# A fused attention and expert kernel: three loads moved to another queue, and smaller shares for background work

## The chip, the core and the metric

The kernel runs on one core of a Trainium2 chip. The core has five engines, each with its own queue of instructions that it works off in order: TensorE (PE in the profile; PEld is its loading of weights), VectorE (DVE), ScalarE (ACT), GpSimd (POOL) and SyncE (SP), which here only issues DMAs. Engines wait for each other and for DMAs through semaphores. The metric is the device time of one execution in microseconds (us), lower is better.

## The reference

Eight sequences of 1024 tokens with 256 features go through a block of causal attention with 16 heads of 16 features, and then through a layer of eight experts, of which each token takes two. Cut to what is computed:

```python
def attn(x, Wq, Wk, Wv, Wo):
    q, k, v = (heads(x @ W.T) for W in (Wq, Wk, Wv))     # 16 heads of 16
    score = where(causal, q @ k.T / sqrt(16), -inf)
    return merge(softmax(score) @ v) @ Wo.T

def ffn(h, router_w, router_b, gate_up, gate_up_b, down, down_b):
    scores = softmax(h @ router_w.T + router_b)          # 8 experts
    topk_w, topk_idx = top_k(scores, 2)
    gate, up = split(h @ gate_up[e] + gate_up_b[e])      # 256 -> 2 x 512
    act = (clip(up, -7, 7) + 1) * min(gate, 7) * sigmoid(1.702 * min(gate, 7))
    y_e = act @ down[e] + down_b[e]                      # 512 -> 256
    return sum over the two chosen experts of topk_w * y_e

x = x + layernorm(attn(layernorm(x)))
x = x + layernorm(ffn(layernorm(x)))
```

All is in float32.

## The kernel before

**Stages.** First comes `begin` (L452): it loads the first sequence (512 KB twice) and W_q, W_k by SP, W_v, W_o by ScalarE's queue (L460), normalises, transposes and projects the first sequence for the first heads, and lets `spread` (L612) copy the heads' 16 rows each into 32-row slots of `qP` and `kP` by small DMAs on SP, four for q and four for k for each half of the sequence. Then the attention runs in 32 units (8 sequences times 4 groups of 4 heads), and then 71 tiles of 256 slots, each of one expert.

**Attention.** A unit passes through two phases. In the first (`maxima_tiles`, PSUM tile `sa`) PE computes scores and VectorE reduces them to row maxima; tokens' maxima go back into a spare row of `qP` (`rows`, L652: `nm`, a transpose `nmps`, a copy `nmT` on ScalarE, four small DMAs on SP). In the second (`values_tiles`, `sb`), PE computes the scores once more, transposed, with the maximum taken off by that spare row, ScalarE exponentiates them (`pT`), GpSimd masks the edges, and PE multiplies with the values (`av`). The first phase of unit u runs beside the second of unit u-1, in 9 steps of 2 pairs of heads. So unit 0 has only the first phase. Two PSUM buffers hold the `sa` of two pairs; a step's kind is EDGE (two masked reductions with the causal mask), TWO (one reduction of a short row of blocks, and a copy of the edge blocks) or WHOLE (one reduction of 1024 columns a partition).

**Background.** All other work (normalising the next sequence, projections `pjq`, `pjk`, values `vps`, the output projection `finish`, and the way of finished tokens to the experts, `route`) is written as generators that yield pieces with costs for the four engines. `pump` gives each engine a credit (`earn`) and emits pieces while no credit they need is below zero (`affordable`). The call for unit 0 is in L1225: it grants 1.2 us of PE per pair. All engines but GpSimd keep the order that the source puts out. `finish_by` at the start of unit 1 emits what is left of the first values and projections; `finish_all` (in the loop over tiles, at tile 10) emits all that is left.

**Where the moved loads stand.** `others` (L523) is such a generator; its first part runs as soon as it is started, after `begin`. There SP issues the router's weight `rwr`, the experts' first biases `gubr`, and four copies of the router's bias `rbias`, then a fill of an empty row block and, later, the bias table. Next it emits `weights` for v and o, then the transposes `rps` (of `rwr`) and `gubps` (of `gubr`) on PE, each with a copy on VectorE.

**Routing.** `route` normalises the tokens (`xn`), transposes them (`x2ps`), multiplies with the router (`lpsT`), transposes back (`lps`), ranks the experts on VectorE, counts with two matmuls (`cps`), and scatters the tokens by 8 indirect DMAs on GpSimd into one region of DRAM per expert. After the last of the 16 token blocks `fill_tails` writes eight fills on SP and `table` computes which tile belongs to which expert (matmuls `segps`, `firstps`, `tabps`). A first table, made when four blocks are still missing, serves tiles 0 to 11 (`EARLY = 12`), so these start before the last blocks are routed; the last two blocks' `finish` and `route` run between the pieces of tiles 0 to 9.

**A tile.** `load_tile` (two tiles ahead) loads rows, weights and biases by SP. `turned` transposes the rows (`xtps`), and each of four quarters does four matmuls into `gu`, `gate` and `up` on VectorE, `sig` on ScalarE, a product on GpSimd, and `act` on VectorE, one quarter late. `lower_half` multiplies with the second weight (`dn`, after the second and the third quarter of the next tile), adds the bias (`ys`) and scatters the result by two indirect DMAs on GpSimd. `pump` is called twice in each quarter (L1310, L1321) and once after it (L1472). At the end `both` gathers, weights, normalises and stores.

Of the kernel before, what the change touches and what calls it, by code (L numbers as in the profile page):

```python
# [11 lines left out]
F32 = mybir.dt.float32  # L12
# [5 lines left out]
P = 128  # L18
# [40 lines left out]
def attn_moe_kernel(  # L59
# [15 lines left out]
    nc = tc.nc  # L75
    B, S, D = x.shape
# [10 lines left out]
    E = router_w.shape[0]  # L87
    FF = down.shape[1]
    FT = FF // P
    TB = 512  # L90
    NT = B * S // TB
    NTB = TB // P
# [44 lines left out]
        out=lower, in_=lower, compare_op=ALU.is_gt, fill=0.0,  # L137
# [270 lines left out]
    with ExitStack() as attn:  # L408
# [43 lines left out]
        def begin():  # L452

            wr = {}
            for name, w, queue, tag in (
                ("q", wq, nc.sync, "avs"), ("k", wk, nc.sync, "avs"),
                ("v", wv, nc.scalar, "aT"), ("o", wo, nc.scalar, "aT"),
            ):
                wr[name] = ap2.tile([P, KT, D], F32, tag=tag, name=f"wr_{name}")
                queue.dma_start(out=wr[name], in_=w.rearrange("(t p) i -> p t i", p=P))  # L460
            xt = xs[0]
            xnTs[0] = ap0.tile([P, KT, S], F32, tag="xnT", name="xnT_0")
            steps = [ln_steps(xt[:, ts(t, NTB), :], NTB) for t in range(NC)]

            def all_of(gen):
                while True:
                    try:
                        next(gen)
                    except StopIteration as end:
                        return end.value  # L470

            def apply(t, mv, rstd):
                shift = small.tile([P, NTB], F32, tag="shift", name="shift")
                nc.vector.scalar_tensor_tensor(
                    shift, mv[:, :, 0:1].rearrange("p n c -> p (n c)"), -1.0, rstd,
                    ALU.mult, ALU.mult,
                )
                xn = ap3.tile([P, NTB, D], F32, tag="xn", name=f"xn_0_{t}")
                for n in range(NTB):
                    of = xt[:, t * NTB + n, :]  # L480

                    if n % 2 and t == 0:
                        ln_apply(xn[:, n, :], of, mv, rstd, n)
                    else:
                        nc.scalar.activation(
                            xn[:, n, :], of, AF.Identity,
                            bias=shift[:, n : n + 1], scale=rstd[:, n : n + 1],
                        )
                return xn

            for name in ("q", "k"):
                uns[0, 0, name] = ap0.tile(
                    [P, S], F32, tag=f"un{name}0", name=f"un{name}_0_0"
                )
            fill(0)
            got = all_of(steps[0])
            for kt in range(KT):
                weights("q", wr["q"], kt)
            for _ in range(NTB // 2):
                next(steps[1])  # L500
            xn = apply(0, *got)
            got = all_of(steps[1])
            for kt in range(KT):
                weights("k", wr["k"], kt)
            for kt in range(KT):
                turn_x(0, 0, xn, kt)
            xn = apply(1, *got)
            for t in range(NC):
                if t:
                    for kt in range(KT):  # L510
                        turn_x(0, t, xn, kt)
                for name in ("q", "k"):
                    project_chunk(0, 0, name, t)
                spread(0, ts(t, QC))
            for mx in mxs:
                in_order(nc.gpsimd.memset(mx, NEG))
            for vp in vps:
                in_order(nc.gpsimd.memset(vp, 1.0))
            for i in range(1, NU):
                fill(i)  # L520
            return wr

        def others(wr):  # L523

            rwr = ap2.tile([E, D], F32, tag="xT", name="rwr")
            nc.sync.dma_start(out=rwr, in_=router_w)
            gubr = ap2.tile([E * 2 * FT, P], F32, tag="xT", name="gubr")
            nc.sync.dma_start(out=gubr, in_=gate_up_b.rearrange("e (c p) -> (e c) p", p=P))
            for n in range(NTB):
                nc.sync.dma_start(out=rbias[:, n, :], in_=router_b.partition_broadcast(P))  # L530

            nc.sync.dma_start(
                out=xs_dram[ds(E * R, TS), :].rearrange("(n p) d -> p n d", p=P), in_=zeros
            )
            for name in ("v", "o"):
                for kt in range(KT):
                    yield piece(pe=0.3, act=0.45)
                    weights(name, wr[name], kt)
            yield piece(pe=0.3, dve=0.2)
            ps = ps_b.tile([P, KT, E], F32, tag="b", name="rps")  # L540
            for kt in range(KT):
                nc.tensor.transpose(ps[:, kt, :], rwr[:, ts(kt, P)], ident[:E, :E])
            nc.vector.tensor_copy(rw32[:, :, :E], ps)
            yield piece(pe=0.2, dve=0.4)
            ps = ps_b.tile([P, E * 2 * FT], F32, tag="b", name="gubps")
            nc.tensor.transpose(ps, gubr, ident[: E * 2 * FT, : E * 2 * FT])
            bias = ap2.tile([P, E, 2 * FT], F32, tag="lgT", name="bias")
            nc.vector.tensor_copy(bias, ps.rearrange("p (e c) -> p e c", e=E))

            nc.vector.tensor_scalar(bias[:, :, FT:], bias[:, :, FT:], 1.0, None, ALU.add)  # L550
            nc.sync.dma_start(
                out=bias_dram[:, :, : 2 * FT].rearrange("e p c -> p e c"), in_=bias
            )
            for e in range(E):
                nc.sync.dma_start(
                    out=bias_dram[e, :, 2 * FT :], in_=down_b[e].partition_broadcast(P)
                )
# [577 lines left out]
        with tc.manual_schedule(  # L1135
# [11 lines left out]
            for u in range(B * NG + 1):  # L1147
# [12 lines left out]
                for k in range(K):  # L1160
# [15 lines left out]
                    for pair in range(2):  # L1176
# [45 lines left out]
                        if first and second:  # L1222
                            pump(most=0.0 if whole and not pair else 1.0)
                        elif first:
                            pump(1.2, 1.2, 0.8, 1.0)  # L1225
                        else:
                            pump(1.2, 2.0, 0.8, 1.4)
                second = values_tiles(u) if first else None
# [69 lines left out]
    def quarter(i, f, xT, wg, bs, act):  # L1298

        ps = ps_gu.tile([P, 2, TS], F32, tag="gu", name=f"gu_{i}_{f}")  # L1300
        for half in range(2):
            for kt in range(KT):
                nc.tensor.matmul(  # L1303
                    ps[:, half, :],
                    lhsT=wg[:, kt, ds(half * FF + f * P, P)],
                    rhs=xT[:, kt, :],
                    start=(kt == 0), stop=(kt == KT - 1),
                )
            if half == 0 and i + AHEAD < EARLY:
                pump(0.6, 0.5, 0.8, 0.6)  # L1310
        gt = m3.tile([P, TS], F32, tag="gate", name=f"gate_{i}_{f}")
        nc.vector.tensor_scalar(gt, ps[:, 0, :], bs[:, f : f + 1], LIMIT, ALU.add, ALU.min)  # L1312
        sg = m3.tile([P, TS], F32, tag="sig", name=f"sig_{i}_{f}")
        nc.scalar.activation(sg, gt, AF.Sigmoid, scale=ALPHA)  # L1314
        up = m3.tile([P, TS], F32, tag="up", name=f"up_{i}_{f}")
        nc.vector.tensor_scalar(  # L1316
            up, ps[:, 1, :], bs[:, FT + f : FT + f + 1], LIMIT + 1.0, ALU.add, ALU.min
        )
        in_order(nc.gpsimd.tensor_tensor(sg, sg, gt, ALU.mult))  # L1319
        if i + AHEAD < EARLY:  # L1320
            pump(0.6, 0.5, 0.8, 0.6)  # L1321

        def product():
            nc.vector.scalar_tensor_tensor(  # L1324
                act[:, f, :], up, 1.0 - LIMIT, sg, ALU.max, ALU.mult
            )

        return product
# [100 lines left out]
    with tc.manual_schedule(engines={engines.PE, engines.DVE, engines.Activation}):  # L1429
# [18 lines left out]
        for i in range(NTILES):  # L1448
# [7 lines left out]
            for f in range(FT):  # L1456
                now_left = quarter(i, f, xT, wg, bs, act)
                if left:
                    left()
                left = now_left  # L1460
                for _ in range(2 if f == FT - 1 and i % 2 else 1):
                    an_end(i)
                if f == 1 and behind:
                    next(behind)
                if f == 2:
                    if i + 1 < NTILES:
                        xTs[i + 1] = turned(i + 1, loads[i + 1][0])
                    if behind:
                        next(behind)
                        next(behind)  # L1470
                if i + AHEAD < EARLY:
                    pump(1.2, 1.0, 1.5, 1.2)  # L1472
            while ready < NT and i >= tiles_for(ready):
                waiting.append(ready)
                ready += 1
# [49 lines left out]
```

## Time and profile before

| | us |
|---|---|
| median of 3 runs | 2242.74 (2240.94 to 2247.95) |
| the profiled execution's own time | 2242.13 |
| its span in the trace | 2240.4 |
| PE busy | 2172.7 (97%) |
| VectorE busy | 1646.1 (73%) |
| ScalarE busy | 1090.1 (49%) |
| GpSimd busy | 1065.0 (48%) |

The span runs from the first to the last instruction. The profile divides it into 40 slices of 56.0 us; unit 0's first `sa` starts at 22.70 us, tile 0's `xtps` at 1413.60 us. A steady tile takes 10.80 us from one `xtps` to the next.

How to read it: a line of the timeline has the start in us, the time in us, engine, source line, operation, result and operands, shapes and count, and in brackets how long the engine had been idle before it and what released it. A line of the windows has the busy time of each engine in a stretch, the granted clock of PE as a share of full speed, and what the DMA engines did. A name like `SPq` means that SP's queue issues a DMA. float32 matmuls run as two passes, so a written matmul counts twice in the trace.

### The profile page before, as it was taken

Reading aid. Unit: us, or ns where it says so; the run is one execution under the profiler, and the core shown is the slowest. Engines: PE = TensorE matmul, PEld = TensorE weight load, DVE = VectorE, ACT = ScalarE, POOL = GpSimd, SP = SyncE. Lnnn points to the kernel's source line nnn. Section 1 sums busy time; section 2 is a strip of 40 time slices with the busy share of each in tenths; the row PEclk is TensorE's granted clock in tenths of the full one; section 3 lists DMA queues with packets and bytes.
Section 4 is the critical chain, followed back from the end, with each engine's and each line's share of the span. In section 5 each row is a group of like instructions: output and inputs, shape, how many; then the busy total and the mean of one; then the engine's idle time right before and its main releaser. Section 6 shows DMA issues by size and latency. Waiting matters only on the chain.

```text
span 2240.4 us, 45184 instructions
## 1 busy us (share of the span) xinstructions
PE 2172.7 (97%) x16801; PEld 1356.0 (61%) x16801; DVE 1646.1 (73%) x3770; ACT 1090.1 (49%) x2179; POOL 1065.0 (48%) x1229
## 2 busy tenths in 40 slices
PE   7999999999999999999999999989999999999995
PEld 4444544544445445445445444678888888888884
DVE  3766777867777877877776787676658888887775
ACT  3566665666666666666666666422112322332222
POOL 3321553573473473472482463464445444454543
PEclk8899999999999999999999999999999999999998
DMA  3101102102111111111111111575567878877773
GB/s 82 38 4 40 22 20 59 40 21 53 37 29 38 51 30 34 51 35 26 51 42 21 47 51 40 205 230 207 201 219 264 274 252 272 275 243 274 242 245 121
DMA packets 141363, 251.17 MB, mean 112 GB/s; under 512 B 17664, under 2 KB 103576, under 8 KB 139224
## 3 DMA queue, kind: packets, MB, share of 16 engines
q1 hardware_dynamic: 127640, 212.22, 30.5%
q0 software_dynamic: 12960, 35.54, 4.2%
q8 instruction: 133, 2.18, 0.4%
q14 instruction: 86, 0.70, 0.1%
q10 hardware_dynamic: 544, 0.52, 0.1%
HBM read 175.74 MB, written 55.76 MB: 103 GB/s over the span
## 4 chain that ended last, share of the span: by engine, by line
PE 83%; DVE 8%; POOL 4%; issue 2%; ACT 1%; DMA 1%; SPq 1%; ACTq 0%; DVEq 0%; POOLq 0%
PE sa L689 20%; PE gu L1303 18%; PE av L821 12%; PE dn L1334 9%; PE sb L784 7%; PE vps L582 3%; PE yps L882 3%; PE pjk L596 3%; PE pjq L596 2%; PE avt L852 1%; PE xtps L1283 1%; DVE acc L1386 1%; POOL pT L801 1%; DVE gate L1312 1%; PE aps L872 1%
## 5 line engine op out<-in xcount | busy, mean ns | idle before, releaser
L792 ACT ACTIVATE pT<-sb 128x512 f32<-128x512 f32 x1152 | 625.0, 595 | 409.7 <-PE sb L784 380.1
L784 PE MATMUL sb<-qP,kP 32*128 32x512 f32 (+3 forms) x3072 | 712.0, 523 | 2.0 <-ACT pT L792 0.8
L689 PE MATMUL sa<-kP,qP 32*128 32x512 f32 (+3 forms) x3072 | 659.7, 527 | 3.2 <-DVE mx L699 1.4
L1303 PE MATMUL gu<-xsT,wg 128*128 128x256 f32 x2272 | 518.6, 381 | 0.7 <-ACT xsT L1285 0.7
L1303 PEld LDWEIGHTS gu<-xsT,wg 128*128 128x128 f32 x2272 | 432.9, 191 | 60.1 <-ACT xsT L1285 1.1
L801 POOL TENSOR_SCALAR_AFFINE_SELECT pT<-pT 128x512 f32<-128x512 f32 x256 | 159.6, 639 | 594.6 <-ACT pT L792 589.2
L1314 ACT ACTIVATE sig<-gate 128x256 f32<-128x256 f32 x284 | 118.3, 416 | 568.1 <-DVE gate L1312 565.2
L705 DVE TENSOR_REDUCE mx<-sa 128x2 f32<-128x1024 f32 x256 | 311.7, 1218 | 112.8 <-PE sb L784 108.7
L821 PE MATMUL av<-pT,vpad 128*32 128x256 f32 (+1 forms) x5120 | 345.0, 366 | 1.1 <-DVE avs L832 0.9
L689 PEld LDWEIGHTS sa<-kP,qP 32*128 32x128 f32 x3072 | 230.5, 185 | 189.8 <-issue 98.7
L1319 POOL TENSOR_TENSOR sig<-sig,gate 128x256 f32<-128x256 f32 x284 | 210.3, 742 | 279.7 <-ACT sig L1314 277.8
L784 PEld LDWEIGHTS sb<-qP,kP 32*128 32x128 f32 x3072 | 298.8, 184 | 40.0 <-ACT pT L792 7.5
L821 PEld LDWEIGHTS av<-pT,vpad 128*32 128x32 f32 x5120 | 116.3, 108 | 287.2 <-issue 209.1
L1334 PE MATMUL dn<-wd,act 128*128 128x256 f32 x1136 | 273.5, 382 | 8.3 <-DVE act L1324 7.8
L1312 DVE TENSOR_SCALAR gate<-gu,bs 128x256 f32<-128x256 f32 x284 | 135.7, 478 | 158.6 <-PE gu L1303 142.6
L1334 PEld LDWEIGHTS dn<-wd,act 128*128 128x128 f32 x1136 | 209.5, 191 | 39.9 <-DVE act L1324 14.6
L699 DVE CUSTOM_DVE_ANT_0 sa<-sa,cmask 128x512 f32<-128x512 f32 x256 | 178.1, 697 | 52.1 <-PE sb L784 27.4
L1344 POOL DMA_INDIRECT ytd<-ys,places x142 | 142.5, 1004 | 134.8 <-DVE ys L1340 109.2
L1042 POOL DMA_INDIRECT xsd<-xn,slots x128 | 126.3, 986 | 49.4 <-issue 30.3
L714 DVE TENSOR_REDUCE mx<-sa 128x2 f32<-128x512 f32 x128 | 88.2, 689 | 79.9 <-PE sb L784 49.7
L1324 DVE SCALAR_TENSOR_TENSOR act<-up,sig 128x256 f32<-128x256 f32 x284 | 130.3, 459 | 18.2 <-POOL sig L1319 18.2
L1316 DVE TENSOR_SCALAR up<-gu,bs 128x256 f32<-128x256 f32 x284 | 134.5, 473 | 0.0
(204 smaller groups left out, 2402.6 us busy)
## 6 DMA issues: line engine op xcount, KB each, us to landing
wg<-_L_ffn_gate_up_proj_dram SPq DMA_DIRECT2D x71, 1024.0 KB
wd<-in_L_ffn_down_proj_dram SPq DMA_DIRECT2D x71, 512.0 KB
xs<-xsd SPq DMA_DIRECT2D x67, 258.0 KB
yy<-ytd SPq DMA_DIRECT2D x15, 1024.0 KB
bs<-biasd SPq DMA_DIRECT2D x71, 132.0 KB
x<-in_L_attn_x_dram SPq DMA_DIRECT2D x16, 512.0 KB
x1d<-y SPq DMA_DIRECT2D x16, 512.0 KB
x<-x1d SPq DMA_DIRECT2D x16, 512.0 KB
```

The lines of the kernel that those rows point to most:

```text
L689: nc.tensor.matmul(ps[:, hh, ds(at, w)], lhsT=qP[r, ts(i, P)], rhs=kP[r, ds(c * QC, w)], start=True, stop=True,)
L699: nc.vector.tensor_tensor_reduce(out=ps[:, hh, :], in0=ps[:, hh, :], in1=cmask, scale=1.0, scalar=NEG, op0=ALU.add, op1=ALU.max, accum_out ...
L705: nc.vector.tensor_reduce(mx[:, heads, i, 2:3], ps, AX.X, ALU.max)
L784: nc.tensor.matmul(banks[hh][:, ds(at, QC - off)], lhsT=kP[r, ts(j, P)], rhs=qP[r, ds(c * QC + off, QC - off)], start=True, stop=True,)
L792: nc.scalar.activation(pT[:, 2 * pair + hh, :], banks[hh], AF.Exp)
L801: in_order(nc.gpsimd.affine_select(out=d, in_=d, compare_op=ALU.is_ge, fill=0.0, base=0, pattern=[[0, HG], [1, P]], channel_multiplier=-1,))
L821: nc.tensor.matmul(av[ds(hh * HS, HS), ds(off + a - at, z - a)], lhsT=vp[:, j, ds((g * HG + hh) * VS, HS)], rhs=pT[:, hh, a:z],  start=c n ...
L1303: nc.tensor.matmul(ps[:, half, :], lhsT=wg[:, kt, ds(half * FF + f * P, P)], rhs=xT[:, kt, :], start=(kt == 0), stop=(kt == KT - 1),)
L1312: nc.vector.tensor_scalar(gt, ps[:, 0, :], bs[:, f : f + 1], LIMIT, ALU.add, ALU.min)
L1319: in_order(nc.gpsimd.tensor_tensor(sg, sg, gt, ALU.mult))
L1334: nc.tensor.matmul(ps[:, n, :], lhsT=act[:, f, ts(n, P)], rhs=wd[:, f, :], start=(f == 0), stop=(f == FT - 1),)
L1344: put = nc.gpsimd.indirect_dma_start(out=yt_dram[:, :], out_offset=bass.IndirectOffsetOnAxis(ap=places[:, i, n : n + 1], axis=0), in_=y[:, ...
```

## The change

Three things are edited. The six loads `rwr`, `gubr` and `rbias` (four times) leave `others`, where SP issued them, and go to `begin`, behind W_v and W_o, on ScalarE's queue; they are handed on in `wr`. The PE share of the background in unit 0 goes from 1.2 to 0.9. The shares in the tiles get smaller: in each quarter's two calls VectorE 0.5 to 0.35, ScalarE 0.8 to 0.6 and GpSimd 0.6 to 0.35; in the call behind a quarter VectorE 1.0 to 0.7, ScalarE 1.5 to 1.0 and GpSimd 1.2 to 0.7; those of PE stay. The credits' order is PE, VectorE, ScalarE, GpSimd.

```diff
@@ begin
                 wr[name] = ap2.tile([P, KT, D], F32, tag=tag, name=f"wr_{name}")
                 queue.dma_start(out=wr[name], in_=w.rearrange("(t p) i -> p t i", p=P))
+
+            wr["r"] = ap2.tile([E, D], F32, tag="xT", name="rwr")
+            nc.scalar.dma_start(out=wr["r"], in_=router_w)
+            wr["gub"] = ap2.tile([E * 2 * FT, P], F32, tag="xT", name="gubr")
+            nc.scalar.dma_start(
+                out=wr["gub"], in_=gate_up_b.rearrange("e (c p) -> (e c) p", p=P)
+            )
+            for n in range(NTB):
+                nc.scalar.dma_start(out=rbias[:, n, :], in_=router_b.partition_broadcast(P))
@@ others
-            rwr = ap2.tile([E, D], F32, tag="xT", name="rwr")
-            nc.sync.dma_start(out=rwr, in_=router_w)
-            gubr = ap2.tile([E * 2 * FT, P], F32, tag="xT", name="gubr")
-            nc.sync.dma_start(out=gubr, in_=gate_up_b.rearrange("e (c p) -> (e c) p", p=P))
-            for n in range(NTB):
-                nc.sync.dma_start(out=rbias[:, n, :], in_=router_b.partition_broadcast(P))
+            rwr, gubr = wr["r"], wr["gub"]
@@ the loop over units
                         elif first:
-                            pump(1.2, 1.2, 0.8, 1.0)
+                            pump(0.9, 1.2, 0.8, 1.0)
@@ quarter, both calls
-                pump(0.6, 0.5, 0.8, 0.6)
+                pump(0.6, 0.35, 0.6, 0.35)
@@ the loop over tiles
                 if i + AHEAD < EARLY:
-                    pump(1.2, 1.0, 1.5, 1.2)
+                    pump(1.2, 0.7, 1.0, 0.7)
```

## The prediction

> **What bounds the kernel.** I read the slices first, then the windows of the two places that stand out, then their waits and timeline.
>
> ```profile
> PE   7999999999999999999999999989999999999995
> PEclk8899999999999999999999999999999999999998
> ```
>
> TensorE (PE) is busy in nearly every slice, so a microsecond (us) by which it starts later or idles is a microsecond of the end. Its granted clock is below full in the first two slices (56 us each); the weak slice 28 is where the first expert tiles run. The windows of the start (columns: stretch, length, busy us of PE, PEld, DVE, ACT, POOL, then PEclk, DMA share, GB/s):
>
> ```profile
> 24.00:29.00 5.00, 0.48 (x3) 0.45 (x3) 1.69 (x5) 0.00 (x0) 0.00 (x0) 0.74 0.17 41
> 29.00:32.00 3.00, 3.00 (x7) 1.29 (x8) 1.13 (x4) 0.00 (x0) 0.00 (x0) 0.50 0.05 3
> 36.00:40.00 4.00, 4.00 (x11) 2.52 (x8) 0.69 (x1) 0.59 (x1) 0.00 (x0) 0.50 0.54 74
> 40.00:44.00 4.00, 4.00 (x32) 2.77 (x32) 1.29 (x2) 2.30 (x4) 1.09 (x1) 0.99 0.74 178
> 60.00:64.00 4.00, 2.80 (x16) 0.74 (x14) 3.01 (x3) 0.41 (x1) 0.00 (x0) 0.99 0.95 159
> 64.00:68.00 4.00, 4.00 (x10) 1.01 (x8) 3.02 (x3) 0.00 (x0) 0.00 (x0) 0.50 0.13 21
> ...
> 26.22 0.53 SPq L526 DMA_DIRECT2D rwr<-L_ffn_router_weight_dram  x1
> ...
> 28.04 0.35 PE L542 MATMUL rps<-ident,rwr 8*128 8x8 f32 x2 [4.21 <-DMA rwr<-L_ffn_router_weight_dram]
> ```
>
> PE stands from 23.8 to 28.0 for the router's weight, which SP issues at 26.22, behind the 16 copies of `spread` (16.07 to 26.2). It goes on only at half clock: from the shares, half clock holds from about 26.4 to 40.1, and once more from 63.9 to 77.6: 13.7 us each. The second follows a stretch with no background matmul left, where PE waits for VectorE's reductions (1.24 us each against 1.06 of PE).
>
> The first expert tiles, by the waits from 1413 to 1512 (total, times, longest) and the timeline:
>
> ```profile
> PE dn L1334 <- DVE act L1324: 3.7, 2, 2.7
> PE cps L1001 <- DVE chosen L997: 3.3, 2, 3.1
> PE tabps L343 <- DVE two L340: 2.3, 1, 2.3
> PE x2ps L940 <- ACT xn L917: 2.1, 4, 1.6
> ...
> 1425.91 0.60 PE L1283 MATMUL xtps<-ident,early 128*128 128x128 f32 x4
> ...
> 1490.13 0.73 POOL L1319 TENSOR_TENSOR sig<-sig,gate 128x256 f32<-128x256 f32 x1
> 1490.89 0.42 DVE L1324 SCALAR_TENSOR_TENSOR act<-up,sig 128x256 f32<-128x256 f32 x1 [3.97 <-POOL sig L1319]
> ...
> 1512.59 0.60 PE L1283 MATMUL xtps<-ident,xs 128*128 128x128 f32 x4
> ```
>
> `xtps` marks tiles 1 and 7. Six steady tiles take 6 x 10.80 = 64.8 (1512.59, 1523.39, 1534.18 are later marks). One half of a `dn` (1.7) does not exist between tiles 1 and 2; the last tokens' own matmuls add 6.6 (x2ps 2.3, lpsT 1.1, cps 1.2, tabps 0.8, the rest 1.2). So 69.7 are due and 86.7 pass: **17.0 us are lost**, 11.4 as waits of the kinds listed, the rest by a third and fourth spell at half clock (from 1491, from 1504.7).
>
> **The start, step by step.** Six loads (L526 to L530) leave SP, 6 x 0.51 = 3.1 us there, and are issued by ScalarE behind its two weight loads at 0.79 and 1.30. That costs ScalarE about 3.1 us from 1.85, and more, because the built program reuses eight DMA semaphores: the last two `rbias` loads now wait for the two halves of x, and on SP wr_q's issue waits for wr_v and wr_k's for wr_o. Behind `rbias` on ScalarE is the table load (1.28, at 1.89 before), then `wqT` at 9.60. x's first half lands at 5.77; the second I put at 7.0 to 7.9, since DMA is full until 8.5 with W_q and W_k last. The table is then ready at 8.8 to 9.7: hidden, or 0.1 late. wr_q was issued at 1.84 but its bytes queue behind x anyway; issued at about 5 (an estimate: wr_v's 256 KB at half of the windows' 340 to 380 GB/s from 2.2 on, and the way to landing) it lands near the old 8.87. The added 56 KB are 0.2 us of bandwidth at 350 GB/s. Bounds: 0 and 2 us; I take **+0.5**, near 0 because bandwidth, not issue, sets the landing.
>
> Gone is the wait 23.8 to 28.0. `rps`, `gubps` follow `sa` at once (0.5). Next in line are heads 2 and 3 of the first `spread`, issued by 21.12; a load takes 1.93 from issue to landing (the row of gubr), so they are there at 23. Then I walk the new order at full-clock prices: sa 1.06, vps 1.92, pj 1.91. From 22.70: 18 pairs of sa 19.1, four vps 7.7, four pj 7.7, small ones 0.8. The even share (0.9 instead of 1.2) puts `vps_3` one step later and the last pj behind `sa_7_0` instead of `sa_5_1`; each WHOLE reduction then has a pj beside it until step 7. VectorE's 24 us of unit 0 fit. New waits on the way: `nmps_0` 0.9 (an EDGE pair's reductions take 1.6), two waits for a reduction at the end 0.6. Unit 0 ends at 59.5, with the shift 60.0, against 68.2.
>
> What is late next is the row maxima's way: `sa_8_1`'s reduction 1.3, `nm` 0.2, `nmps` 0.4, ScalarE 1.3 (two exps first), four issues at 0.64 (2.6), landing 2.0, hand-overs 0.3: 8.1. The first `sb` of step 2 waits for them: 68.1, against 77.7 before, where half clock covered that way. **Start: -9.6.** The 1.4 us by which this is more than the gain at 68.2 is the covered piece.
>
> [...] The row says that 2.4 us of the stop pass before SP even issues, behind copies that wait for projections; the order is what changes. [...]
>
> [...] The rows differ: at 63.9 the clock fell after a longest gap of 1.2 us (PE 70% busy in 60 to 64). [...] A spell of 13.7 us costs at most 6.85, about 5 where other engines hold PE anyway. I take no fall (a window at 48 to 52 was 71% busy without one) and keep 5 for the range.
>
> **The first tiles.** In the built order the last tokens' way ends (`tabps`) in tile 8 instead of 6, still before `finish_all` at tile 10, so nothing is dumped there. Shares per tile fall from 8.0 to 5.6 us of VectorE, from 9.6 to 5.6 of GpSimd. With its own work (VectorE 6.7; GpSimd 4 x 0.74 + 2 x 1.27 = 5.5) each had been given 15 in a tile of 10.8; now 12.3 and 11.1. By wait:
> - x2ps (2.1): its four `xn` now stand a gu before it; lpsT follows its two copies (1.1) closely: 1.2 left.
> - cps (3.3): `chosen` is ahead of the next gate now; 0.5 left.
> - dn (3.7): five scatters of 1.27 stood before one `sig`. Now one or two per quarter, but all 16 in tiles 4 to 7: from tile 4's `sig_2` to tile 7's, 12 x 0.74 + 22 x 1.28 = 37 us of GpSimd in about 34 of PE. Walking it, `dn` of tile 4 waits 1.3, later ones find their `sig` done 0.5 us ahead. 1.5 left.
> - tabps: the same nine small VectorE operations (2.5 us) against half a gu: 2.3 stay.
> - half clock: by the rows it needed a wait of about 3 us; none is left, so 0, or 3 to 5 if it falls.
>
> Left 5.5 of 17.0: **-11.5**. In tile 0 half a gu now covers the wait for `atok` (0.7): -0.5. The eight zero fills (8.2 us of SP) stand behind tile 9's loads; tile 10's weights then wait 8 of their slack of some 16 us. Between ends for this part: -4 (GpSimd holds and the clock falls twice) and -16.
>
> **Sum.** -9.6 - 12.0 = -21.6 on the profiled execution's 2242.1 (span 2240.4 and 1.7 around it), which is 0.6 below the median of 2242.7. Forecast **2221**.
>
> **Rivals.** A change below 0.3% (6.7 us) can't be told from none here.
> - Forecast, both gains: 0.62, 2214 to 2229.
> - The clock falls in the new kernel where the row allows it, at 60 to 68 or at tiles 4 to 7, but not both fully: one spell takes 5, GpSimd's lag 3 more: 2229. For it: the fall at 63.9; against: shorter waits. 0.20.
> - Only one part works (the maxima's way or ScalarE's waits eat the start, or VectorE's order still breaks the tiles): 2231 to 2233. 0.10.
> - Nothing to see, the moved loads' stop taken over by the next wait, and tiles GpSimd-bound: 2240. 0.04.
> - Slower: GpSimd in tiles 4 to 7. If its lag passes about 2.7 us per tile, PE stands that long at each `dn` and the clock falls each time, as it did after 1488.6. Four spells at 6.85 and the left 5.5 make 33 where 17 were lost: +16, less 9.6: 2248. My count of the lag is 1.3. 0.04.
>
> Range 2213 to 2234. Faster 0.92, same 0.04, slower 0.04.
>
> **What would show it.** `rps` right behind the first `sa`, near 24.5, with no wait on a DMA; PEclk 1.00 from 24 to 60; `sb` of unit 1 step 2 near 68. From tile 1's `xtps` to tile 9's about 97 us instead of 108.3; `dn` waits under 1.5, `tabps` 2.3 unchanged. Wrong if `wqT` starts past 11, if PEclk shows 0.50 in 60 to 80, or if `sig` waits for scatters at every tile.

## The result and the profile after

The changed kernel takes **2227.97 us** (median of 4 runs, 2226.80 to 2229.58) beside 2242.64 (4 runs, 2240.94 to 2247.95) for the kernel before: ratio **0.9932, 95% interval 0.9918 to 0.9947**, so 14.7 us faster. The forecast was 21.6. The profiled execution took 2227.21, 14.9 less than that of before, and this is what the times below split up. Tile 0 starts 9.6 us earlier, tile 0 to tile 9 is 5.5 us shorter; behind tile 10 nothing changes.

The slices of the changed kernel's page; in the kernel before the first two digits of PEclk were 8:

```profile
PE   7999999999999999999999999999999999999995
PEclk9999999999999999999999999999999999999998
```

Its start, in the windows view (columns as in the prediction), shows full clock from 24 on, but not to 60:

```profile
24.00:29.00 5.00, 4.88 (x23) 2.85 (x23) 2.81 (x10) 1.26 (x5) 0.00 (x0) 1.00 0.22 52
...
40.00:44.00 4.00, 2.04 (x6) 0.76 (x5) 2.72 (x7) 0.73 (x2) 0.00 (x0) 0.80 0.60 150
44.00:48.00 4.00, 4.00 (x18) 1.45 (x17) 1.01 (x2) 0.87 (x2) 0.00 (x0) 0.77 0.08 15
...
60.00:64.00 4.00, 4.00 (x16) 2.24 (x18) 3.18 (x9) 1.21 (x3) 0.00 (x0) 0.50 0.05 10
64.00:68.00 4.00, 3.99 (x35) 2.75 (x29) 3.54 (x11) 2.26 (x5) 0.64 (x1) 0.71 0.02 4
```

Half clock holds from about 42.4 to 45.8 and from 59.5 to 66.3: 10.2 us, where the kernel before had 27.3. The timeline of the start:

```profile
3.12 5.35 ACTq L469 DMA_DIRECT2D rbias<-n_L_ffn_router_bias_dram  x4
5.45 0.37 SPq L460 DMA_DIRECT2D wr_q<-in_L_attn_Wq_dram  x1
...
11.40 0.81 ACT L447 ACTIVATE wqT<-wps_q 128x256 f32<-128x256 f32 x2 [1.62 <-PE wps_q L446]
...
24.77 1.13 PE L693 MATMUL sa<-kP,qP 32*128 32x512 f32 x4
25.73 0.23 PE L546 MATMUL rps<-ident,rwr 8*128 8x8 f32 x2
...
68.46 0.48 PE L788 MATMUL sb<-qP,kP 32*128 32x256 f32 x1
```

The stop of 4.21 us before `rps` is gone: no bracket, right behind `sa`. But W_q is issued at 5.45 instead of 1.84, its transposes start at 10.71 instead of 8.90, and the first `sa` at 24.77 instead of 22.70. The last line is the first `sb` of unit 1's step 2, which needs the row maxima of unit 0: 68.46 instead of 77.58.

The tiles, by their `xtps` (tiles 0, 1 and 9 here) and by PE's waits from 1404 to 1519 (total, times, longest):

```profile
1404.04 0.66 PE L1288 MATMUL xtps<-ident,early 128*128 128x128 f32 x4 [0.81 <-DVE avs L836]
1415.50 0.60 PE L1288 MATMUL xtps<-ident,early 128*128 128x128 f32 x4
...
1519.08 0.60 PE L1288 MATMUL xtps<-ident,xs 128*128 128x128 f32 x4
```

```profile
PE cps L1005 <- DVE chosen L1001: 3.1, 2, 2.1
PE dn L1339 <- DVE act L1329: 2.9, 3, 1.4
PE tabps L343 <- DVE two L340: 2.1, 1, 2.1
PE segps L311 <- DVE new L304: 1.2, 1, 1.2
PE lpsT L951 <- ACT xT L945: 1.0, 1, 1.0
```

Tile 1 to tile 9 takes 103.6 us (before 108.3, forecast 97). The clock stays full, but the waits are hardly less than before.

**Idle and clock apart.** A stretch can be split with the windows view in steps of 1 us: idle is the length less PE's busy time; clock loss is busy time times (1 - PEclk). From 22 to 84 us idle falls from 7.4 to 4.8 and clock loss from 12.6 to 5.1. From tile 0 to tile 10, which is 131.4 before and 125.8 after, idle falls from 12.7 to 11.3 and clock loss from 4.6 to 0. Idle and clock loss together fall by 16.1 us in the two stretches, and 12.1 of them are clock that no longer falls; the first `sa`'s delay of 2.1 us works against this.

### The profile page after: what moved, and what is told of

It is laid out like the page before. It is cut to its first block, busy times and chain, and to the rows that moved or that the text cites. A ratio compares the mean times of both kernels' runs of the same rounds, so it can differ in the third digit from the quotient of the medians.

```text
span 2225.5 us, 45180 instructions
## 1 busy us (share of the span) xinstructions
PE 2161.5 (97%) x16801; PEld 1347.5 (61%) x16801; DVE 1647.3 (74%) x3770; ACT 1090.8 (49%) x2179; POOL 1067.0 (48%) x1229
## 4 chain that ended last, share of the span: by engine, by line
PE 81%; DVE 10%; POOL 4%; issue 3%; ACT 1%; DMA 1%; SPq 0%; ACTq 0%; DVEq 0%; POOLq 0%
PE sa L693 20%; PE gu L1308 17%; PE av L825 12%; PE dn L1339 9%; PE sb L788 7%; PE yps L886 3%; PE pjq L600 3%; PE pjk L600 3%; PE vps L586 2%; PE avt L856 1%; DVE acc L1391 1%; PE xtps L1288 1%; DVE gate L1317 1%; DVE act L1329 1%; DVE up L1321 1%
```

## The experiments

Times stand beside the kernel before on the same chip: it takes 2278.16 us on the chip of the first four runs, 2277.16 on that of the next four, and 2242.89 on that of the last. On the first two chips the executions of one kernel are up to 18 us apart, and go with the mean granted clock (over 45 executions of the kernel before, -1.6 us per thousandth of the clock, correlation -0.87): in the trace of run 3 the clock falls in the attention too (0.97 to 0.99 in six of the thirteen stretches of 100 us from 100 to 1400, where the first trace of before has 1.00 in all). The clock is not all of it: in these 1300 us PE also idles for 18.2 us there, beside 10.0 and 9.7 in the traces of before and after. So verdicts rest on ratios, and explanations on stretches.

**1. Only the loads are moved**, shares as before.

```diff
+  (begin) nc.scalar.dma_start(out=wr["r"] | wr["gub"] | rbias ...)
-  (others) nc.sync.dma_start(out=rwr | gubr | rbias ...)
```

> Only the loads are moved; unit 0's share and the tiles' shares are those of before. If the gain at the start comes from PE no longer standing for the router's weight: first sa 2 us late (24.8), rps right behind it, no half clock from 26 to 40, tile 0's xtps near 1406 to 1408 instead of 1413.6, and the same 120.6 us from there to tile 9; time near 2236. If the even share makes the gain instead: tile 0 not before 1411, time 2240 or more.

Measured: ratio 0.9978 (0.9968 to 0.9988), 2271.73 us. First `sa` at 25.31, with no stop behind it; the first `sb` of step 2 starts at 68.10, beside 76.89 in run 3, whose loads are those of before.

**2. Only unit 0's share.**

```diff
-  pump(1.2, 1.2, 0.8, 1.0)
+  pump(0.9, 1.2, 0.8, 1.0)
```

> Only unit 0's PE share goes to 0.9. If the loads carry the gain: the stop from 23.8 to 28.0 and the half clock after it stay, the later one near 64 gets shorter or goes, tile 0 near 1411, time 2239 to 2241. If the even share carries it: tile 0 near 1406, time near 2235.

Measured: 0.9999 (0.9987 to 1.0011). `rps` still waits 4.08 us for its DMA.

**3. Only the tiles' shares.**

```diff
-  pump(0.6, 0.5, 0.8, 0.6)      pump(1.2, 1.0, 1.5, 1.2)
+  pump(0.6, 0.35, 0.6, 0.35)    pump(1.2, 0.7, 1.0, 0.7)
```

> Only the tiles' shares are smaller. Theory: the 5.5 us that the whole change gained between tile 0 and tile 9 are all from here and come from the half clock that is gone, so tile 0 to tile 9 takes 115 instead of 120.6, with waits of PE that sum to as much as before; time near 2237. Rival: these 5.5 us were a matter of when the tiles begin, and the stage takes 119 or more; time 2241 or more.

Measured: 0.9965 (0.9952 to 0.9978); tile 0 to tile 9 takes 116.5 us, with one fall of the clock (1.7 us lost). The parts add up: 0.22% and 0.35% make 0.57%, and the whole change on a chip of the same speed (run 5) has 0.53%. In microseconds the loads are worth 5.0 (2.7 to 7.3) by these medians and the shares 8.0 (5.0 to 10.9), where the traces of the first result have 9.6 and 5.5 for the two places; the start by itself is 8.8 shorter in the traces of runs 1 and 3 too. Why the median of run 1 shows less than that is open.

**4. The whole change, but `rbias` stays on SP.** Eight loads are then issued at the start instead of twelve, x, W_q and W_k among them.

```diff
-  (begin)  for n in range(NTB): nc.scalar.dma_start(out=rbias[:, n, :], ...)
+  (others) for n in range(NTB): nc.sync.dma_start(out=rbias[:, n, :], ...)
```

> The whole change, but the four rbias loads stay on SP where they were, so that only eight DMAs come before the first semaphore is used again. If the later landing of W_q (10.7 instead of 8.9) is the wait for W_v's load, W_q lands at 8.9 again, the first sa starts near 22.8, and the time is 2 us below that of the whole change, near 2226. If the extra bytes on ScalarE's queue delay it: W_q still at 10 or later, same time as the whole change.

Measured: 0.9941 (0.9925 to 0.9957). Its timeline:

```profile
1.83 0.51 SPq L460 DMA_DIRECT2D wr_q<-in_L_attn_Wq_dram  x1
1.88 0.65 ACTq L463 DMA_DIRECT2D rwr<-L_ffn_router_weight_dram  x1
```

W_q is issued at 1.83 again and its transposes start at 8.81 instead of 10.50 (run 1); the first `sa` starts at 23.23 instead of 25.31. Two waits of SP in the changed kernel, which the kernel before and run 4 do not have, show the reason, and the windows from 7 to 8 us (first the changed kernel, then before) show that it is not bandwidth:

```profile
SPq L460 <- DMA wr_v<-in_L_attn_Wv_dram: 3.6, 1, 3.6
SPq L460 <- DMA wr_o<-in_L_attn_Wo_dram: 2.2, 1, 2.2
...
7.00:8.00 1.00, 0.00 (x0) 0.00 (x0) 0.90 (x5) 0.00 (x0) 0.45 (x1) 1.00 0.32 55
7.00:8.00 1.00, 0.00 (x0) 0.00 (x0) 0.93 (x4) 0.00 (x0) 0.44 (x1) 1.00 1.10 347
```

The issues of W_q and W_k wait until W_v and W_o have landed, loads whose data they do not use. The changed kernel's trace gives the semaphores: its first eight loads have one each, 100 to 107, and the other four take 100 to 103 again, each after a wait on it; W_q's is 100, that of W_v, and W_k's is 102, that of W_o. The DMA engines are a third busy from 7 to 8 us (0.32) instead of full (1.10). So the reuse of DMA semaphores delayed the start by 2.1 us.

**5. The changed kernel on the second chip.** No edit.

> The changed kernel itself, so that it stands beside the others on one chip. Theory: its ratio to before is 0.993 again, tile 0 to tile 9 takes about 115 us, and the last two `rbias` loads on ScalarE and W_q's issue on SP still wait for DMA semaphores that are used again: W_q lands near 10.6, the first `sa` starts near 24.8. Rival: the gain belonged to one chip; then the ratio lies above 0.997.

Measured: 0.9947 (0.9928 to 0.9965), 2264.86 us; W_q at 10.42, first `sa` at 24.52. Tile 0 to tile 9 took 116.7 in this execution: the same waits as in the first result, and one fall of the clock (1.7 us lost, from 1547).

**6 and 7. One engine's shares in the tiles back to those of before.** First VectorE's, then GpSimd's:

```diff
-  pump(0.6, 0.35, 0.6, 0.35)    pump(1.2, 0.7, 1.0, 0.7)
+  pump(0.6, 0.5, 0.6, 0.35)     pump(1.2, 1.0, 1.0, 0.7)    (run 6)
+  pump(0.6, 0.35, 0.6, 0.6)     pump(1.2, 0.7, 1.0, 1.2)    (run 7)
```

> The whole change, but VectorE's shares in the tiles as before (0.5 and 1.0). Theory 1, VectorE's own backlog makes PE's waits for `chosen` and `act`: most of the tiles' gain is lost again, tile 0 to tile 9 takes 118.5 to 120.5 instead of 115, and the time is 3 to 5 us above the changed kernel's. Theory 2, GpSimd's scatters ahead of `sig` made them: 115 to 116, and the time as the changed kernel's.

> The whole change, but GpSimd's shares in the tiles as before (0.6 and 1.2). Theory 1 (VectorE): tile 0 to tile 9 stays at 115 to 116.5. Theory 2 (GpSimd's scatters ahead of `sig`, and then VectorE's `act` waits for `sig`): 118.5 to 120.5, with several us of `act` waiting for `sig`, and 3 to 5 us more time.

Measured: run 6 0.9947 (0.9927 to 0.9968), tile 0 to tile 9 117.3 us; run 7 0.9984 (0.9973 to 0.9995), 122.2 us. GpSimd's share carries the tiles' gain (8.8 us between runs 7 and 5): with it back, the ratio is that of run 1, which has none of the new shares, within the intervals. VectorE's carries none that can be measured, and theory 1 falls; ScalarE's was not tried apart, and run 7 leaves little for it. Theory 2's sign came, `act` waits 7.0 us for `sig` in run 7 (3.2 in the changed kernel), but little of it reaches PE: PE waits 3.2 us before `dn`, hardly more than the changed kernel's 2.9, its idle from tile 0 to 10 is 11.5 against 11.3, and in run 8 below `act` waits 8.6 us for `sig` without harm. The windows of run 7 show what differs:

```profile
1513.71:1519.71 6.00, 2.85 (x15) 2.24 (x13) 5.70 (x15) 0.83 (x2) 4.90 (x6) 0.90 0.81 264
1519.71:1525.71 6.00, 6.00 (x17) 4.91 (x18) 3.67 (x16) 0.42 (x1) 5.17 (x6) 0.53 0.50 187
```

PE idles 3.15 of these 12 us in one piece, before `cps`, and then works at half clock. Four such spells, behind waits of 2.0 to 3.2 us, cost 8.0 us; run 6 has two (3.4 us).

**8. PE's pieces held back.** Loads as in run 4; the generator's `after`, the least number of calls of pump behind the piece before, goes up for the last tokens' way.

```diff
-  more = 1 if last else 0                       # lpsT, lps, cps: after=1 + more
+  more = 3 if last else 0
-  yield piece(pe=0.6, dve=0.2, after=3)         # segps
+  yield piece(pe=0.6, dve=0.2, after=3 if first_ones else 4)
-  yield piece(pe=0.5, dve=0.6, after=2)         # tabps
+  yield piece(pe=0.5, dve=0.6, after=2 if first_ones else 4)
```

> The changed kernel with the four `rbias` loads left on SP, and in the last tokens' way PE's pieces (`lpsT`, `lps`, `cps`, `segps`, `tabps`) are held back one to two calls of pump longer behind the VectorE or ScalarE work that they read. Theory A, what is left of the loss in the tiles is PE arriving too soon at these few matmuls (cps 3.1, tabps 2.1, segps 1.2, lpsT 1.0 of the changed kernel's waits): these fall to under 2 together, tile 0 to tile 10 is 4 to 6 us shorter, and together with the start (first `sa` near 23.2) the time is 5 to 8 us below the changed kernel's. Rival B, VectorE is simply behind there, and a later piece only moves the wait to `dn`: tile 0 to tile 10 changes by less than 2, the time by 2 to 3 for the start alone.

Measured: 0.9912 (0.9885 to 0.9938), 2254.65, 10.2 below run 5's median (the intervals overlap). Tile 0 to tile 10 takes 120.6 instead of 125.8 (127.5 in run 5). Theory A holds, for less idle and for the tiles' time; the waits of this stretch:

```profile
PE dn L1339 <- DVE act L1329: 3.6, 4, 1.2
PE cps L1005 <- DVE chosen L1001: 1.0, 1, 1.0
...
PE tabps L343 <- DVE two L340: 0.5, 1, 0.5
```

`dn` waits 0.7 more; `cps`, `tabps`, `segps`, `lpsT` and `firstps` together 5.5 less (1.9 instead of 7.4).

**9. Idle filled in the kernel before.** Matmuls of no use stand before three of its waits:

```diff
+  for f in range(6 if i == 4 and n == 0 else 0):   nc.tensor.matmul(ps[:, 0, :], ...)   # dn
+  for k in range(7 if len(routed) == NT - 1 else 0): nc.tensor.matmul(wide[:, D:], ...) # cps
+  for k in range(0 if first_ones else 9):          nc.tensor.matmul(wide[:, D : ...], ...) # tabps
```

> The kernel before, with matmuls of no use put in front of three of the last tokens' waits in the tiles (7 before the second `cps`, 6 before `dn` of tile 4, 9 before the second `tabps`; some 2.3 to 2.9 us each, of 128 rows, into parts of PSUM tiles that are overwritten or not read). No wait gets shorter; PE is only busy in it. Theory C, the tiles' gain of the change is the clock that no longer falls: no window of the tiles below 0.97, tile 0 to tile 10 at 126 to 127.5 us, as in the changed kernel, where the kernel before has 131.4 and its copies with the same tiles 133.3 and 133.8; ratio to before 0.996 to 0.998. Rival D, the gain is shorter waits: tile 0 to tile 10 stays at 131 or above, ratio 1.000 or more.

Measured: 0.9993 (0.9985 to 1.0001), tile 0 to tile 10 132.5 us: theory C's numbers are missed, and rival D's are met within the interval. The timeline shows why this does not decide between the two:

```profile
1443.01 0.33 PE L946 MATMUL x2ps<-ident,xn 128*128 128x128 f32 x1 [1.65 <-ACT xn L923]
...
1492.09 0.70 PE L1350 MATMUL dn<-wd,act 128*128 128x256 f32 x2 [0.18 <-DVE act L1335]
...
1501.83 0.58 PE L319 MATMUL firstps<-seg,before 128*128 128x1 f32 x2 [2.97 <-DVE seg L316]
```

Before `dn` the fall of the kernel before (from 1490.7) is gone, although `act` comes no earlier. But the clock fell at two waits that were not filled: at 1443, where the kernel before waits 1.6 us too and keeps its clock, and at 1501, where the wait stands at `firstps` and so ahead of the fill, as it does in runs 1 and 2 without any fill (3.0 us). In this trace the fill removes the fall where it stands; that the clock is what the tiles gained is not shown by it.

**10, 11, 12. Unit 0, from run 8's kernel.** Run 10 fills two waits, 5 matmuls before `nmps_0` and 2 before the last `sa`; run 11 sets the share back to 1.2; run 12 is run 8's kernel as the measure.

```diff
+  for k in range(5 if not u and not c else 0): nc.tensor.matmul(wide[:, P:], ...)       # run 10
+  if not u and (k, pair) == (K - 1, 1): fill = ...; 2 x nc.tensor.matmul(fill, ...)     # run 10
-  pump(0.9, 1.2, 0.8, 1.0)                                                              # run 11
+  pump(1.2, 1.2, 0.8, 1.0)                                                              # run 11
```

> The lagged version (rbias on SP) with 5 matmuls of no use before `nmps_0` and 2 before unit 0's last `sa`, where PE waits 1.97 and 1.32 us. Theory: both spells at half clock (some 42 to 46 and 59 to 70) are gone, since only the low activity made them; of the 6.8 us of clock loss about 1.5 was on the path at the first, the second stands beside the row maxima's way, which ends near 67 anyway; so tile 0 comes 1.5 to 3 earlier than in the lagged version of the same chip. Rival 1: 5 or more (all of the clock loss was on the path). Rival 2: the clock falls all the same, and nothing changes.

> The lagged version with unit 0's share of PE back at 1.2. The prediction's argument, that 0.9 is needed to keep a projection beside every late reduction: then 2 to 4 us later than the lagged version at the first `sb`, with a longer spell at half clock after 57. Rival: the share only moves the waits (1.2 less before `nmps_0`, more among the last `sa`): within 1 us of the lagged version.

> The lagged version once more, as the measure for the two before on this chip: ratio to before 0.991 (0.9885 to 0.9938 before), tile 0 to tile 10 at 120.6, no fall of the clock in the tiles.

Measured: run 10 2218.61 us, 0.9890 (0.9875 to 0.9905); run 11 2222.56, 0.9914 (0.9899 to 0.9928); run 12 2221.14, 0.9900 (0.9885 to 0.9915). Run 10's windows, where the changed kernel has 0.80 and 0.50:

```profile
40.00:44.00 4.00, 4.00 (x18) 1.87 (x20) 1.02 (x4) 1.04 (x3) 0.00 (x0) 1.00 0.55 145
...
60.00:64.00 4.00, 3.39 (x34) 1.84 (x38) 3.83 (x15) 2.42 (x6) 0.63 (x1) 1.00 0.03 8
```

With the waits filled the clock does not fall (clock loss from 22 to 84 is 0.0 instead of 5.1, and in the traces of the changed kernel and of runs 4, 5, 8 and 12 both spells are there, 17.1 us apart), so low activity of PE made both. The medians differ by 2.5 us, within what was expected, but the intervals overlap. By the traces the first `sb` of step 2 starts at 65.28 instead of 66.31, although the fill itself holds `nmps_0` until 41.77 instead of 40.08. Run 11 lies within 1.5 of run 12, with intervals that overlap, and the argument that 0.9 is needed is not borne out. Its trace even speaks against it: with 1.2, PE waits 1.2 us before `nmps_0` instead of 2.0, and the first of the two spells is not there. From the first `sa` to the first `sb` of step 2, runs 1 and 11 take 42.8 and 42.7 us, and the seven traces with the share of 0.9 and the moved loads take 43.7 to 44.0. Run 12's profiled execution had 5.1 us of clock loss in the attention, which run 11's had not, so its tile 0 is not set beside the others. Tile 0 to tile 10 takes 120.5 to 120.6 in all three, with no fall.

On the last chip, as fast as that of the first result, the interval of the version of runs 8 and 12 (0.9885 to 0.9915) lies below the changed kernel's 0.9918 to 0.9947 of the first result, though the changed kernel itself was not run there; on the second chip the two intervals overlap. The version with the fill can't be told from it.

## Why the prediction was right, point by point

The direction and the two places were right, the gain came out a third below the forecast, and the start was met by luck, with errors that cancel. Two of the prediction's own three signs of being wrong came true: `wqT` starts at 11.40, past 11, and PEclk shows 0.50 in 60 to 64. What happened is nearer to its second case, a fall of the clock at 60 to 68 (2229, chance 0.20), than to its forecast of 2221.

- **The stop before `rps`**: right. It is gone, and `sa` goes on at full clock. Run 1 shows that the moved loads alone do it, run 2 that the share alone does nothing.
- **The start shift, put at +0.5 with bounds 0 and 2**: it was +2.1. The prediction saw that W_q's issue waits for a semaphore, and its "about 5" for the issue was near (5.45), but it held that bandwidth sets the landing. Run 4 and the idle DMA engines from 7 to 8 us show that the issue does.
- **No fall of the clock from 24 to 68**: wrong. It fell at 42.4 and 59.5. The row of before (a fall behind a longest gap of 1.2 us) foretold this better than the choice that was made: the longest gaps ahead of the two falls were 1.96 and 1.31. Its price was put at about 5. Run 10's median is 2.5 lower without both spells, which is not clear of noise; how much of the second the row maxima's way would have covered is not shown.
- **18 pairs of `sa` at 1.06, 19.1 us**: they took 13.9 (the differences of the starts in the timeline). Two lines of the changed kernel's timeline show the error:

```profile
29.08 1.14 PE L693 MATMUL sa<-kP,qP 32*128 32x128 f32 x8
...
32.07 1.16 PE L693 MATMUL sa<-kP,qP 32*128 32x128 f32 x16
```

  Eight matmuls are a pair here, sixteen are two, and they take the same time: pairs that follow each other directly, on different 32-row slots, run side by side (in the trace the second pair's first matmul starts at 32.10, while the first pair's runs from 32.07 to 32.44). Of the seven places where two pairs follow each other, five take 1.1 to 1.2 us and two some 2. The price per pair held only where something stands between them.
- **Unit 0's end, 60.0**: 59.5. Shift +1.6, `nmps_0` +1.1 (1.96 instead of 0.9), the first spell +1.7, the last waits +0.7 make 5.1 too little; the `sa` are 5.2 too much. Behind it the prediction let the row maxima's way decide. The first `sb` of step 2 is near its forecast (68.46, forecast 68.1), but PE works without a gap from 59 on, at half clock until 66.3, so a wait for the maxima is not seen. So the start's -9.6 stands in the trace as forecast, by a sum whose terms were not.
- **The first tiles, -12.0**: the term that was mis-sized; measured -5.5. The half clock's part (5.6 to 0) was 4.6 to 0 in this execution, with some luck: runs 3 and 5 have the very same waits and lose 1.7 each to one fall. The waits' part was wrong: `cps` was put at 0.5 and waits 3.1, `dn` at 1.5 and waits 2.9, `segps` was not counted and waits 1.2; `tabps` (2.3, measured 2.1) and `lpsT` (1.2, measured 1.0) were right. The sentence that failed is "`chosen` is ahead of the next gate now". The timeline of the changed kernel:

```profile
1478.12 0.42 DVE L994 TENSOR_REDUCE rank<-ge 128x32 f32<-128x256 f32 x1
1478.46 0.47 DVE L1317 TENSOR_SCALAR gate<-gu,bs 128x256 f32<-128x256 f32 x1
...
1480.29 0.17 DVE L1001 TENSOR_SCALAR chosen<-rank 128x32 f32<-128x32 f32 x1
...
1480.61 0.38 PE L1005 MATMUL cps<-chosen,before 128*128 128x32 f32 x2 [2.13 <-DVE chosen L1001]
```

  A `gate`, an `up` and an `act` stand between `rank` and `chosen`; before, a `gate` and an `up` did. The shares set how much work is handed out per quarter; how far PE's piece stands behind VectorE's is set by `after`, which the change leaves alone. Idle from tile 0 to 10 is 12.7, 11.3, 10.5 and 11.5 for the shares of before, after, run 6 and run 7; only the `after` of run 8 brings it to 6.4. The clock loss in the profiles is what follows the shares: 4.6, 7.3 and 5.9 in the three with the old ones (before, runs 1 and 2), 0, 1.7, 0 and 1.7 in the four with the new (after, runs 3 to 5), 3.4 with VectorE's back and 8.0 with GpSimd's. That this is because the same idle falls in smaller pieces (longest wait 2.1 instead of 3.1) is argued from these rows, not tried apart, and how GpSimd's share does it is open.
- **GpSimd as the bound in tiles 4 to 7 (the slower rival)**: not seen. PE's waits at `dn` are 1.4 at the longest, where the rival needed more than 2.7 at each, and the clock stays full. The count of 1.3 for tile 4's `dn` (measured 1.45) was close.
- **The loads' move, read from the row of `rwr`**: right. Run 1 has 0.22% (0.12 to 0.32) for it, since the issue of `rwr` moves past what SP had queued ahead of it (1.88 instead of 26.22).

## What to carry to other kernels

Split a lossy stretch into idle and clock loss before you price a change: here a wait of 2 to 3 us on PE costs itself, and often 1.7 us or more besides, as half clock behind it. One execution does not show that price, since the same wait had a fall behind it in one trace and none in the next. If background work stalls the engine that bounds, look at how far a piece stands behind its producer, and not only at how much work is granted per step. Before you move loads to an idle queue, count the DMAs that are under way: here twelve loads shared eight semaphores, W_q's issue waited 3.6 us for a load of another queue, and with eight loads (run 4) it did not wait.

## What was not expected of the hardware

In the traces, spells at half clock begin and end on a grid of about 3.41 us that runs on through one execution: in the kernel before, 26.4 to 63.9 is 11 steps and 26.4 to 1490.7 is 429. The spells before the end last four, four, two and one steps there, one and two in the changed kernel, and one to four in the start and the tiles of the runs.

In the tiles, the share of such a step in which PE was busy goes with what follows. The 17 falls there, in eight traces (before and runs 1 to 3, 5 to 7 and 9), came behind steps of 0.09 to 0.47 and one of 0.58; every step up to 0.45 was followed by one, and none of 0.66 or more was. So it counts where a wait lies on the grid. The longest of the kernel before, 3.09 us in front of `cps` from 1471.8, is shared by two steps of 0.46 and 0.63, and the clock stays; those of 2.75 and 2.26 lie mostly in one step each (0.39 and 0.44), and it falls behind both. The two waits of 2.1 us in the changed kernel's tiles stand in four traces, and two of these eight have a fall behind them.

The share does not decide everywhere. In the attention of run 12 the clock fell behind steps of about 0.70 and 0.77 (at 958.4 and 1135.9), and in runs 1 and 11 it fell in the start behind 0.76 and 0.77. Nor does a busy step always bring the clock back: at 29.8 to 40 and 64 to 77 of the kernel before it took three and four steps at 1.00. Both are open.
